# Order of the weight looks, turning steps of the second batch's x, and place of the third gated filler in an attention and ternary FFN kernel

## The chip, the cores and the metric

The kernel runs on one core of one Trainium2 chip. The metric is the device time of one execution in microseconds; each kernel is judged by the median of several timed runs. A separate execution was taken with the hardware profiler; its lines are quoted below. PE is the matrix engine, PEld its weight loads, DVE the vector engine, ACT the scalar engine, POOL the general engine, and SP the engine whose queue issues most of the DMA transfers.

## What is computed

The input x has 2 sequences of 2048 rows with 256 features, in fp32. One layer is computed, attention and FFN side by side on the normalised input:

```
xn = layernorm(x)
q, k, v = xn @ Wq, xn @ Wk, xn @ Wv
attn = softmax(causal(q @ k.T) * 256 ** -0.5) @ v @ Wo
h = silu((xn @ w1.T) * w1_s) * ((xn @ w2.T) * w2_s)      # 1024 wide
h = gelu((h @ h1.T) * h1_s)
h = gelu((h @ h2.T) * h2_s)
out = x + attn + (h @ w3.T) * w3_s
```

The FFN weights w1, w2, h1, h2 and w3 are ternary: each entry is -1, 0 or 1. The kernel doesn't assume this but looks at every weight, and has a second, general FFN for the case that a look finds something else.

## The kernel before

**Blocks.** The rows are cut into 8 blocks n of 512 rows (0 to 3 are the first sequence, 4 to 7 the second), each into 4 tiles t of 128 rows. Matmul operands are kept in two parts, a rounded high part and the remainder, the low part, so one product is three matmuls.

**Attention** runs first, tile by tile. `score(n, t, m)` (L428 to L449) multiplies tile (n, t) by the keys of block m, adds the causal mask (L434), takes the row maximum on DVE (L437) and, after the last m, the exponential on ACT (L449). The weights must then be transposed. Where at least five 128-column tiles lie together this is done off PE: a DVE transpose of 32x32 blocks into one of two b buffers (`turn_blocks`, L308), a DMA write to DRAM called d (L313), and four DMA fetches (`fetch_blocks`, L320) that put the blocks in place, into one of two buffers called e. `turn` then makes the high part (ACT, L487) and the low part (DVE or POOL in turn, L489) from e; otherwise it transposes on PE (L493). `weigh(n, t, m)` (L519, L524) multiplies by the values, and scales on ACT (L539) and adds on POOL (L540) after the last m.

**The order** of this work is written out by a planner. It counts each PE step in units of one matmul column group (a product of six 512-column matmuls is 3,072 units), goes through 34 steps j, and in step j merges the scores of tile j and the extra work listed for j with the weighing of an earlier tile. Steps 0 to 15 are the tiles of blocks 3 down to 0, steps 16 to 31 those of blocks 4 to 7; steps 32 and 33 only weigh. The tile framework then orders each engine's instructions by its own simulated time, so an instruction can run ahead of its place in the program; `issue_after` holds one behind another.

**Keys.** For the first sequence x is normalised and transposed on PE. For the second, `turn_keys(n)` does it ahead: four ACT activations normalise the block (L343), one DVE transpose (L308, x into b), one DMA write (d_x, L313) and four fetches back into x (L320) turn it. `keys(n)` later casts it into the key tile (ACT L366), subtracts the low part (POOL L367) and stores the keys to DRAM (xT_d, L368), from where the FFN loads them. `TURN_KEYS` lists the steps at which blocks 4, 5, 6 and 7 are turned. The queries (L385) and values (L401) of blocks 4 to 7 stand in steps 13 to 24.

**Looks.** Each of the FFN weights is looked at in pieces, beside the attention. The list `items` gives the order; `beside(cost)` runs the next step of the list when enough units have gone by since the last (the gap: 8,000 or 11,000 units where the next piece could be loaded ahead, 15,000 where not, because there are two staging buffers and a chunk of h1 takes both). A piece of w1, w2 or w3 takes a DVE bit test (L598) and an ACT sum (L600). A piece of h2 takes an absolute value on ACT (L605) and a comparison on DVE (L607). A chunk of h1 is two pieces: four sums of its quarters on DVE (L155), made in the tile xh0, a store of these (1024 KB, L621), and the test for both. After the last chunk of h1, xh0 is loaded with the keys of block 0 (L618). At attention's end `judge` (L502 to L506) brings all results into one flag, on which the branch to the FFN depends.

**Fillers.** The FFN's first products for block 0 read xh0 and need no attention result, so four of them are used to fill PE at attention's end: `first_quarter(i)`, i = 0 to 2 (8 matmuls at L174 into two PSUM banks, then silu on ACT L182, a product on DVE L183, and the split L187 and L188), and `last_quarter` behind attention's last matmul. The four banks `ps` are taken in turn by scores, fillers and the judge.

**FFN.** `ffn_ternary` goes through pairs of blocks. The two 1024x1024 layers are done by a seven-product scheme on quarters (L886), whose factors for h1 are the sums stored by the looks; the output product is L1047.

Of the kernel before, what the change touches and what calls it, by code (L numbers as in the profile page):

```python
# [21 lines left out]
TB = 512  # L22
NT = TB // P
# [5 lines left out]
Q = 32  # L29
UK = 8  # L30
LEAST = 5
TURN_KEYS = [8, 10, 12, 14]
LOOKS_FROM = 3
LEAD = 2
WARM = 26
# [30 lines left out]
def attn_ffn_kernel(  # L66
# [36 lines left out]
    B, S, D = x.shape  # L103
    H = w1.shape[2]
    NB = S // TB
    N = B * NB
    DC = D // P
    HC = H // P
    SC = 1024
# [81 lines left out]
    with ExitStack() as actx:  # L191
# [20 lines left out]
        def bank():  # L212
            return in_turn("ps", ps_tiles)
# [164 lines left out]
        def queries(n, m):  # L378
            if m == 0:
                qs[n] = in_turn("q", q_tiles)  # L380
            pp = bank()
            k = 0
            for a, b in ((0, 0), (1, 0), (0, 1)):
                for c in range(DC):
                    nc.tensor.matmul(  # L385
                        out=pp, lhsT=wqk[:, c, a, ts(m, P)], rhs=ks[n][:, c, b, :],
                        start=(k == 0), stop=(k == 3 * DC - 1),
                    )
                    k += 1
            hi_lo(qs[n][:, m, 0, :], qs[n][:, m, 1, :], pp)  # L390

        def values(n, half):
            if half == 0:
                vs[n] = vp.tile([P, NT, 2, D], F32R, tag="v", name=f"v_{n}")
            pv = bank().rearrange("p (u d) -> p u d", d=D)
            for u in range(2):
                t = 2 * half + u
                k = 0
                for c in range(DC):
                    for a, b in ((0, 0), (0, 1), (1, 0)):  # L400
                        nc.tensor.matmul(  # L401
                            out=pv[:, u, :], lhsT=ks[n][:, c, a, ts(t, P)], rhs=wvo[:, c, b, :],
                            start=(k == 0), stop=(k == 3 * DC - 1),
                        )
                        k += 1
            v = vs[n][:, ts(half, 2), :, :]
            hi_lo(v[:, :, 0, :], v[:, :, 1, :], pv)
# [90 lines left out]
        def judge():  # L498

            assert not looks  # L500
            most = small.tile([P, 1], F32, tag="most", name="most")
            nc.vector.reduce_max(most, low_bits[:, : looked[0]], axis=AX.X)  # L502
            with tc.issue_after(marks["PE"]):
                pf = bank()
                nc.tensor.matmul(out=pf[:1, :1], lhsT=most, rhs=ones, start=True, stop=True)
            nc.vector.tensor_copy(flag, pf[:1, :1])  # L506

        def weigh(n, t, m):
            if (n, t, m) == (N - 1, NT - 1, N - 1):
                judge()  # L510
            first = n - n % NB
            st = state[n, t]
            if m == first:
                st["po"] = ps_o.tile([P, 2, D], F32, tag="po", name=f"po_{n}_{t}")
            tiles = NT if m < n else t + 1
            pT = st.pop(m)

            for j in range(tiles):
                nc.tensor.matmul(  # L519
                    out=st["po"], lhsT=pT[:, 0, ts(j, P)], rhs=vs[m][:, j, :, :],  # L520
                    start=(m == first and j == 0), stop=False,
                )
            for j in range(tiles):
                marks["PE"] = nc.tensor.matmul(  # L524
                    out=st["po"][:, 0, :], lhsT=pT[:, 1, ts(j, P)], rhs=vs[m][:, j, 0, :],
                    start=False, stop=(m == n and j == tiles - 1),
                ).ins
            if m == n:
                total = small.tile([P, 1], F32, tag="total", name=f"total_{n}_{t}")
                nc.vector.reduce_sum(total, st["sums"][:, : (n - first) * NT // UK + 1], axis=AX.X)  # L530
                inv = small.tile([P, 1], F32, tag="inv", name=f"inv_{n}_{t}")
                nc.vector.reciprocal(inv, total)
                if n not in attn:
                    attn[n] = rp.tile([P, NT + 1, D], F32, tag="r", name=f"r_{n}"), []
                r, made = attn[n]

                up = n < NB
                two = r[:, ds(t, 2), :]
                nc.scalar.activation(two, st["po"], AF.Copy, scale=inv)  # L539
                nc.gpsimd.tensor_tensor(two[:, int(up), :], two[:, 0, :], two[:, 1, :], ALU.add)  # L540
                made.append(t)
                if len(made) == NT:
                    assert made == sorted(made, reverse=up)
                    nc.sync.dma_start(out=r_d[n], in_=r[:, ds(int(up), NT), :].rearrange("p t d -> p (t d)"))
                del state[n, t]
# [23 lines left out]
        def block_steps(n):  # L569
            return [  # L570
                (2 * TB, lambda: keys(n)),
                (6 * TB, lambda: queries(n, 0)),
                (6 * TB, lambda: queries(n, 1)),
                (6 * TB, lambda: values(n, 0)),
                (6 * TB, lambda: values(n, 1)),
            ]
# [15 lines left out]
        def low(tiles, dst):  # L592
            (t,) = tiles
            if dst is not None:
                rounded(dst, t)
            tb = t.bitcast(U32)
            with tc.issue_after(marks["DVE"]):
                nc.vector.tensor_scalar(tb, tb, LOW_BITS, None, ALU.bitwise_and)  # L598
            with tc.issue_after(marks["ACT"]):
                nc.scalar.activation(t, tb, AF.Copy, accum_out=seen())  # L600

        def odd(t):

            with tc.issue_after(marks["ACT"]):
                nc.scalar.activation(t, t, AF.Abs)  # L605
            with tc.issue_after(marks["DVE"]):
                nc.vector.scalar_tensor_tensor(  # L607
                    t, t, 0.0, t, ALU.not_equal, ALU.not_equal, accum_out=seen()
                )
# [19 lines left out]
        def item_low(src, dst):  # L629
            items.append(([src], [(0, lambda t: low(t, dst))]))  # L630

        def item_signs(src):
            items.append(([src], [(0, lambda t: odd(t[0]))]))

        def item_factors(src, f, c):
            steps = [(0, lambda t: sum_up(t, 0))]
            steps += [(2500, lambda t, i=i: sum_up(t, i)) for i in (1, 2, 3)]
            steps += [
                (1500, lambda t: store_sums(f, c)),
                (6000, lambda t: odd(t[0])),  # L640
                (3000, lambda t: odd(t[1])),
            ]
            if c == HK - 1:
                steps.append((0, lambda t: load_xh0()))
            items.append(([src[:, c, :], src[:, c + HK, :]], steps))

        for c in range(HK):
            src, dst = ((w1, w1_sb), (w2, w2_sb))[c // DC]
            item_low(src[:, c % DC, :], dst[:, c % DC, :])
        w3_at = list(range(0, HC, SC // D))  # L650
        for c in range(HK):
            item_factors(h1, factors["h1"], c)
            for k in (2 * c, 2 * c + 1):
                item_signs(h2[:, k, :])
            if c >= 2:
                w = w3_at[c - 2]
                item_low(w3[:, w : w + SC // D, :].rearrange("p c d -> p (c d)"), None)

        def fetched_weights(i):
            for src in items[i][0]:  # L660
# [50 lines left out]
        for k, src in (("w1", w1_s), ("w2", w2_s), ("h1", h1_s), ("h2", h2_s)):  # L711
# [3 lines left out]
        tiles = [divmod(i, NT) for i in range(NB * NT - 1, -1, -1)]  # L715
# [5 lines left out]
        extra = {  # L721
            0: [(6 * TB, lambda: values(0, 0)), (6 * TB, lambda: values(0, 1))],
            2: [(6 * TB, lambda: queries(2, 0)), (6 * TB, lambda: queries(2, 1))],
            6: [(6 * TB, lambda: queries(1, 0)), (6 * TB, lambda: queries(1, 1))],
            10: [(6 * TB, lambda: queries(0, 0)), (6 * TB, lambda: queries(0, 1))],
            13: block_steps(NB)[:3],
            14: block_steps(NB)[3:],
            15: block_steps(NB + 1)[:1],
            16: block_steps(NB + 1)[1:],
# [6 lines left out]
        def first_quarter(i):  # L736

            banks = [bank(), bank()]
            gated_products(banks, xh0, i)
            with tc.issue_after(marks["ACT"]):  # L740
                gated(f_views[i], banks, i)
                split_into(h_views[i], f_views[i])

        extra[len(tiles)] = [(8 * TB, lambda i=i: first_quarter(i)) for i in range(2)]
        extra[len(tiles) + 1] = [(8 * TB, lambda: first_quarter(2))]

        def before(j):
            if 3 <= j < 3 + NB:
# [4 lines left out]
            if j == 3 + NB:  # L753
                with tc.issue_after(marks["ACT"]):
                    r = root(mv1.rearrange("p n t k -> p (n t) k"), NB * NT, "1")
                for i in range(NB):
                    rstds[NB + i] = [a[:, ts(i, NT)] for a in r]
            if j in TURN_KEYS:
                turn_keys(NB + TURN_KEYS.index(j))

# [497 lines left out]
```

## Time and profile before

| What | Value |
|---|---|
| timed runs | 872.51, 873.72, 876.49 us (median 873.72) |
| the profiled execution | 870.29 us, of it the span 868.5 us |
| mean granted PE clock | 0.994 |
| busy in the span | PE 851.4 us, PEld 722.0, DVE 635.6, ACT 512.4, POOL 250.0 |
| DMA | 162.52 MB in 62,678 packets |
| steps 8, 16, 24, 31 scored (L434) at | 99.8, 140.1, 194.8, 254.8 us |
| x of blocks 4 to 7 normalised (first L343) at | 97.95, 117.53, 128.12, 136.81 us |
| the same cast into keys (first L366) at | 115.45, 131.52, 145.44, 158.53 us |
| h1's sums stored (L621) at | 100.37, 152.10, 186.12, 240.71 us |
| last matmul of attention; first FFN product in an own bank | 281.3; 283.2 us |

Times in the profile count from the span's start. In a list of instructions, the columns are the start, the time from the first start to the last end of the merged row, engine, line, operation, the names written and read, the count, and in brackets the idle time before it and what ended it. The busy time of PE includes matmuls that run at a lower granted clock. A stretch of a queue's own engine (SPq) is the time in which it issues.

### The profile page before, as it was taken

To read this page: it belongs to the slowest core of one execution; us is meant where nothing else is said; L and a number is where in the kernel's file an instruction comes from. 1 tells how busy PE (TensorE), PEld (TensorE's weight loads), DVE (VectorE), ACT (ScalarE), POOL (GpSimd) and SP (SyncE) were. 2 spreads that over 40 slices of the span, in tenths; PEclk is the share of its full clock that TensorE was granted. 3 is DMA by queue.
4 is the path that set the end of the run, shared out by engine and by line. 5 is a ranking of instruction groups with operands and counts; after the bars stand their busy time and mean duration, and the time that the engine had idled before them with its cause. 6 is when DMAs were issued, how large, how long until landed. Compare 5 with 4: busy or idle time off the path is not lost.

```text
span 868.5 us, 12281 instructions
## 1 busy us (share of the span) xinstructions
PE 851.4 (98%) x4298; PEld 722.0 (83%) x4298; DVE 635.6 (73%) x1091; ACT 512.4 (59%) x897; POOL 250.0 (29%) x194
## 2 busy tenths in 40 slices
PE   8999998999999999999999999999999999999997
PEld 6988877988887878888988888988888898888887
DVE  6688766776775699996596596579478648848764
ACT  3456677755647456677257586536557635657671
POOL 3033344321322576550142150025024003502300
PEclk9999999999999999999999999999999999999999
DMA  8977899765792998854234444433344431144411
GB/s 280 356 243 241 242 295 283 241 240 190 235 324 63 368 384 309 318 193 145 99 121 150 144 144 143 148 112 112 144 146 145 145 136 57 50 146 145 146 49 53
DMA packets 62678, 162.52 MB, mean 187 GB/s; under 512 B 6544, under 2 KB 36368, under 8 KB 53264
## 3 DMA queue, kind: packets, MB, share of 16 engines
q1 hardware_dynamic: 57792, 145.14, 48.1%
q10 hardware_dynamic: 3728, 12.32, 4.6%
q0 software_dynamic: 1088, 4.19, 1.3%
q8 instruction: 36, 0.59, 0.3%
q14 instruction: 34, 0.28, 0.1%
HBM read 120.21 MB, written 47.71 MB: 193 GB/s over the span
## 4 chain that ended last, share of the span: by engine, by line
PE 74%; DMA 11%; DVE 6%; issue 3%; SPq 2%; ACT 2%; POOL 0%; ACTq 0%; DVEq 0%; POOLq 0%
PE ps_own L886 23%; PE ps L886 22%; PE ps L174 6%; PE ps_own L174 6%; DMA e<-d 5%; PE ps_own L1047 4%; PE ps L1047 4%; PE ps L428 3%; SPq L320 2%; DMA d<-b 2%; PE po L519 2%; PE ps L401 2%; DMA x<-d_x 2%; DVE b L308 1%; PE ps L385 1%
## 5 line engine op out<-in xcount | busy, mean ns | idle before, releaser
L428 PE MATMUL ps<-k,q 128*128 128x512 f32 (+3 forms) x480 | 112.0, 368 | 0.4 <-ACT q L264 0.4
L428 PEld LDWEIGHTS ps<-k,q 128*128 128x128 f32 x480 | 82.5, 191 | 13.5 <-ACT q L264 1.2
L519 PE MATMUL po<-v,pT 128*128 128x512 f32 x272 | 79.4, 404 | 5.1 <-ACT pT L487 3.8
L1018 POOL TENSOR_TENSOR rt<-rt,xt 128x1024 f32<-128x1024 f32 x8 | 21.8, 2744 | 165.3 <-issue 114.8
L907 ACT ACTIVATE k_h_u<-k_h_u,h_s_sb 128x512 f32<-128x512 f32 x64 | 45.9, 723 | 38.5 <-DVE k_h_u L906 37.9
L449 ACT ACTIVATE s<-s,low 128x1024 f32<-128x1024 f32 (+7 forms) x48 | 43.0, 897 | 30.8 <-DVE low L443 30.7
L519 PEld LDWEIGHTS po<-v,pT 128*128 128x128 f32 x272 | 48.1, 191 | 14.0 <-ACT pT L487 4.9
L866 POOL TENSOR_TENSOR k_h_u<-k_h_p,k_h_u 128x512 f32<-128x512 f32 x16 | 23.2, 1452 | 122.8 <-ACT q L187 106.0
L489 POOL TENSOR_TENSOR pT<-e,pT 128x512 fp32r<-128x512 f32 (+3 forms) x30 | 36.2, 1205 | 64.8 <-ACT pT L487 59.6
L487 ACT CAST pT<-e 128x512 fp32r<-128x512 f32 (+3 forms) x60 | 32.5, 573 | 31.9 <-DMA e<-d 26.5
L540 POOL TENSOR_TENSOR r<-r 128x256 f32<-128x256 f32 x32 | 26.5, 829 | 82.9 <-ACT r L539 76.3
L437 DVE TENSOR_SCALAR_CACHE_REDUCE s<-ps 128x512 f32<-128x512 f32 (+3 forms) x80 | 47.2, 598 | 2.7 <-PE ps L428 1.6
L524 PEld LDWEIGHTS po<-v,pT 128*128 128x128 f32 x272 | 42.7, 191 | 7.3 <-DVE pT L489 1.1
L524 PE MATMUL po<-v,pT 128*128 128x256 f32 x272 | 47.7, 287 | 0.7 <-DVE pT L489 0.6
L188 DVE TENSOR_TENSOR q<-k_h_u,q 128x512 fp32r<-128x512 f32 x32 | 45.9, 1463 | 0.0
L308 DVE STREAM_TRANSPOSE b<-s 128x1024 f32<-128x1024 f32 (+3 forms) x30 | 33.7, 1130 | 13.8 <-ACT s L449 12.8
L925 POOL TENSOR_TENSOR k_h_p<-f_h_B,k_h_p 128x512 f32<-128x512 f32 x16 | 34.4, 2179 | 21.2 <-DVE h_h_T L188 21.2
L489 DVE TENSOR_TENSOR pT<-e,pT 128x512 fp32r<-128x512 f32 x30 | 23.4, 781 | 20.7 <-ACT pT L487 20.6
L174 PE MATMUL ps<-xh,w_sb 128*128 128x512 f32 x144 | 36.0, 391 | 1.7 <-ACT b L182 1.7
L866 POOL TENSOR_TENSOR f_w_B<-f_w_B,f_w_B 128x512 f32<-128x512 f32 x16 | 26.8, 1690 | 33.1 <-DVE f_w_B L183 33.1
L906 DVE TENSOR_TENSOR k_h_u<-ps_own,k_h_u 128x512 f32<-128x512 f32 x32 | 21.7, 686 | 17.6 <-PE ps_own L886 17.6
L907 ACT ACTIVATE k_h_p<-k_h_p,h_s_sb 128x512 f32<-128x512 f32 x32 | 22.8, 722 | 18.6 <-DVE k_h_p L906 18.6
(178 smaller groups left out, 2224.4 us busy)
## 6 DMA issues: line engine op xcount, KB each, us to landing
w_h_S<-factors_h SPq DMA_DIRECT2D x32, 1024.0 KB, 4.7
w_h_A<-factors_h SPq DMA_DIRECT2D x24, 1024.0 KB, 4.8
d<-b SPq DMA_DIRECT2D x18, 512.0 KB, 3.5
e<-d SPq DMA_DIRECT2D x72, 128.0 KB, 3.0
xT_d<-k SPq DMA_DIRECT2D x8, 1024.0 KB, 5.5
stg<-in_ffn_h_w ACTq DMA_DIRECT2D x16, 512.0 KB, 5.3
factors_h<-xh SPq DMA_DIRECT2D x4, 1024.0 KB, 4.9
r_d<-r SPq DMA_DIRECT2D x8, 512.0 KB, 5.3
```

What stands on the lines that cost most here:

```text
L174: nc.tensor.matmul(out=p, lhsT=w[:, c, ts(o, P)], rhs=xh[:, c, a, :], start=(c == 0 and a == 0), stop=(c == DC - 1 and a == 1),)
L188: nc.vector.tensor_tensor(r[:, 1, :], f, r[:, 0, :].bitcast(F32), ALU.subtract)
L428: nc.tensor.matmul(out=ps[:, :w], lhsT=qs[n][:, c, a, ts(t, P)], rhs=ks[m][:, c, b, :w], start=(k == 0), stop=(m < n and k == 3 * DC - 1),)
L437: marks["DVE"] = nc.vector.tensor_scalar(st["s"][:, ds(at, w)], ps[:, :w], 1.0, None, ALU.mult, ALU.max, accum_out=st["tops"][:, m - first ...
L449: marks["ACT"] = nc.scalar.activation(st["s"][:, at], st["s"][:, at], AF.Exp, bias=low, accum_out=st["sums"][:, u // UK : u // UK + 1],).ins
L489: engine.tensor_tensor(lo, src, hi.bitcast(F32), ALU.subtract)
L519: nc.tensor.matmul(out=st["po"], lhsT=pT[:, 0, ts(j, P)], rhs=vs[m][:, j, :, :], start=(m == first and j == 0), stop=False,)
L524: marks["PE"] = nc.tensor.matmul(out=st["po"][:, 0, :], lhsT=pT[:, 1, ts(j, P)], rhs=vs[m][:, j, 0, :], start=False, stop=(m == n and j == ...
L866: nc.gpsimd.tensor_tensor(B["B12"][i], B["B22"][i], B["B12"][i], ALU.subtract)
L886: nc.tensor.matmul(out=out[o], lhsT=w[:, c, ts(o, P)], rhs=sets[right][c][:, a, :], start=(start and c == 0 and a == 0), stop=(c == HK - 1 ...
L907: nc.scalar.activation(C[k][o], r[o] if r else banks[o], AF.Gelu, scale=s[:, at : at + 1])
L1047: nc.tensor.matmul(out=ys[t][:, :D], lhsT=h[c][:, a, ts(t, P)], rhs=w3_sb[:, c, :], start=(c == 0 and a == 0), stop=(c == HC - 1 and a == 1),)
```

## The change

Three things change.

1. `TURN_KEYS`: blocks 5, 6 and 7 are turned at steps 9, 10 and 12, where they were turned at 10, 12 and 14. Block 4 stays at 8.
2. The order of `items`: behind the four pieces of w1 and w2 come all eight pieces of h2, then the four chunks of h1, then the two pieces of w3. Before, each chunk of h1 was followed by two pieces of h2, and pieces of w3 stood after the third and the fourth group. The gaps follow from the order: between pieces of h2 the next is loaded ahead.
3. `first_quarter(2)` is called ahead of `weigh(7, 3, 6)`, the last but one; before, it was the first work of step 33, ahead of the weighing of tile (7, 2).

```diff
-TURN_KEYS = [8, 10, 12, 14]
+TURN_KEYS = [8, 9, 10, 12]
...
         def weigh(n, t, m):
+            if (n, t, m) == (N - 1, NT - 1, N - 2):
+                first_quarter(2)
             if (n, t, m) == (N - 1, NT - 1, N - 1):
                 judge()
...
         w3_at = list(range(0, HC, SC // D))
+
+        for k in range(HC):
+            item_signs(h2[:, k, :])
         for c in range(HK):
             item_factors(h1, factors["h1"], c)
-            for k in (2 * c, 2 * c + 1):
-                item_signs(h2[:, k, :])
-            if c >= 2:
-                w = w3_at[c - 2]
-                item_low(w3[:, w : w + SC // D, :].rearrange("p c d -> p (c d)"), None)
+        for w in w3_at:
+            item_low(w3[:, w : w + SC // D, :].rearrange("p c d -> p (c d)"), None)
...
         extra[len(tiles)] = [(8 * TB, lambda i=i: first_quarter(i)) for i in range(2)]
-        extra[len(tiles) + 1] = [(8 * TB, lambda: first_quarter(2))]
```

## The prediction

> **What bounds the kernel now.** I first read the busy time of each engine in stretches, cut where attention ends (281 us) and where each pair of FFN blocks ends.
>
> ```profile
> 88.00:281.00 193.00, 185.43 (x1024) 159.52 (x1024) 137.24 (x327) 124.09 (x235) 61.47 (x61) 0.98 0.75 237
> 424.00:570.00 146.00, 146.00 (x705) 123.28 (x704) 104.23 (x144) 87.18 (x146) 33.02 (x18) 1.00 0.39 137
> 716.00:862.50 146.50, 146.50 (x708) 123.58 (x706) 104.40 (x144) 86.01 (x145) 32.99 (x18) 1.00 0.27 94
> ```
>
> The columns are the stretch, its length, busy time (and count) of PE, PE's weight loads, DVE, ACT and POOL, then PE's granted clock, the DMA share and GB/s. From 424 us on PE never rests, and the diff touches nothing there. So the change can only win or lose PE's idle time and low clock between step 6 (73 us) and the first FFN products. The next view is the same, in finer stretches.
>
> ```profile
> 121.00:125.00 4.00, 2.91 (x13) 1.80 (x12) 3.11 (x8) 3.19 (x7) 0.73 (x1) 1.00 1.03 414
> 140.00:146.00 6.00, 6.00 (x35) 4.99 (x33) 3.10 (x8) 2.36 (x7) 1.71 (x3) 1.00 1.05 307
> 146.00:149.00 3.00, 0.35 (x2) 0.29 (x2) 0.48 (x2) 2.12 (x6) 2.86 (x3) 0.83 0.80 264
> 149.00:155.00 6.00, 6.00 (x25) 5.52 (x25) 5.07 (x15) 2.76 (x7) 1.89 (x3) 0.51 0.96 278
> 165.00:250.00 85.00, 84.72 (x471) 73.41 (x470) 65.56 (x168) 49.98 (x94) 23.48 (x23) 1.00 0.71 230
> 250.00:262.00 12.00, 11.46 (x59) 9.45 (x58) 6.16 (x14) 6.64 (x12) 3.15 (x4) 1.00 1.02 325
> 262.00:266.00 4.00, 2.31 (x15) 1.81 (x14) 2.19 (x6) 3.97 (x8) 0.00 (x0) 1.00 0.53 120
> ```
>
> One place stands out: an idle PE at 146 to 149, and half the clock for six microseconds behind it. To price low clock and short gaps too, I took the time from each matmul's start to the next, less the time that the same shape takes back to back (0.227 us for 512 columns, the 7.25 us per 32 of the FFN; 0.118 for 256). The excess is 2.78 us at 145.7 to 148.6, 2.93 behind it up to 155, 1.88 at 121 to 125, 2.45 in 165 to 250, 0.98 in 250 to 262, 1.74 in 262 to 266. That is nearly all there is to win. Now the queues at the worst place: PE, then ACT, then SP.
>
> ```profile
> 148.71 2.07 PE L519 MATMUL po<-v,pT 128*128 128x512 f32 x4 [2.65 <-ACT pT L487]
> ```
>
> ```profile
> 145.44 1.14 ACT L366 CAST k<-x 128x512 fp32r<-128x512 f32 x2 [3.64 <-DMA x<-d_x]
> 146.48 0.68 ACT L539 ACTIVATE r<-po,inv 128x512 f32<-128x512 f32 x1
> 148.04 0.82 ACT L487 CAST pT<-e 128x512 fp32r<-128x512 f32 x2 [0.88 <-DMA e<-d]
> ```
>
> ```profile
> 134.78 0.34 SPq L368 DMA_DIRECT2D xT_d<-k  x1
> 135.21 4.07 SPq L320 DMA_DIRECT2D x<-d_x  x4
> 139.32 0.49 SPq L544 DMA_DIRECT2D r_d<-r  x1
> 140.63 4.28 SPq L320 DMA_DIRECT2D e<-d  x4
> ```
>
> PE waits for a cast of turned weights, e. ACT first waits for turned x (block 6, turned at step 12), then for e. The fetch of e is late because on SP it stands behind block 5's key store, the four fetches of block 6's x and a result's store, while the DMA engines are full (1.05).
>
> **The change, part by part.** The profiled execution took 870.29 us (span 868.5); the median of the three timed runs is 873.72 (872.51 to 876.49). I sum against 870.29 and carry the difference over to the median.
>
> *Turning x at steps 8, 9, 10, 12.* A turn is four ACT activations (L343, 0.59 each, 2.06 as one row), one DVE transpose (1.24), one SP write of 512 KB and four SP fetches of 128 KB; when they land come two ACT casts (0.62 each), two POOL subtractions (1.42 each) and an SP store of 1024 KB. The planner's counts give block 5 its turn 14,080 units earlier, block 6 14,592, block 7 20,480; at 155 us per 305,152 units between steps 8 and 31 (scored 99.8 and 254.8) that is 7.2, 7.4 and 10.4 us. Block 6 thus takes block 5's old place, block 7 block 6's. The keys aren't needed earlier: their queries (L385) start 9 to 26 us behind the casts. No deadline is won, so what counts is what the transfers collide with.
>
> At 135 to 148 block 7 now stands where block 6 stood, with block 6's store ahead of it. What is gone from there are h1's two loads (issued at 134.96 and 137.55, 512 KB each; one load of h2 stands instead) and block 7's own write at 145. 512 KB less at 307 GB/s bring e in 1.7 us earlier, so 1.1 of the 2.78 us remain. Gaps of 1.07 and 1.70 us, at 123 and 265, left the clock at 1.00 in their stretches, so I take the low clock's 2.93 as gone: **-4.6**. Bounds: 0 (the collision stays) and -5.7 (gone altogether).
>
> The row is all that this rests on; a rule speaks against part of it. The Trainium skill, "TensorE: Matmul & The Clock Gate", section "HAM oscillation — how this bites in real kernels", has it that gaps over about 3.4 us throttle the clock. Here 2.65 us were enough, so by the measurement the gap's length alone doesn't decide. By the rule no gap of this trace would throttle, shortening one would save no clock, and the place would be worth 1.7 instead of 4.6.
>
> Block 5's turn at step 9 is a burst where there was none: ACT is 7.61 of 11 us busy there, the DMA share 0.87 to 0.95. The same burst at 117.5, with a look at 121, goes before the 1.88 us of 121 to 125; at 128 it cost nothing visible. Bounds 0 and +1.9; middle, **+1.0**. The casts and POOL's 2.83 us per block also move: POOL is busy 5.22 of 15 us from 125 to 140, so they cost nothing there; without that cover the lo half behind them (L489) is late by up to 2.83.
>
> *h2's looks first.* The looks' gaps add up to 332,000 units instead of 362,000. The last look is made in step 31 instead of 33, xh0 is loaded at 410,112 instead of 431,360, well before its first use in step 32, and h1's last store at 399,360 instead of 418,816; nobody waits for these. The 1 MB store of sums at 100.4 us moves behind step 16; block 5's x comes into that stretch instead. From step 16 on DVE has 16 sums, 8 odd tests and two low ones (11.0 + 9.8 + 1.6 us) in 216,000 units, where it had 8, 10 and two (5.5 + 12.2 + 1.6) in 271,000: 0.20 of the time instead of 0.14. DVE is at 0.77 from 165 to 250, and 0.9 between 230 and 250 cost PE nearly nothing; bounds 0 and +1.5, I take **+0.3**.
>
> *The end.* There ACT had, in one row, two exps, an abs of a look (1.04), a table load (1.28) and the silu (0.69):
>
> ```profile
> 262.18 1.04 ACT L605 ACTIVATE stg<-stg 128x1024 f32<-128x1024 f32 x1
> 263.24 1.28 ACT L182 ACT_TABLE_LOAD   x1
> 264.53 0.69 ACT L182 ACTIVATE b<-ps,w_s_sb 128x512 f32<-128x512 f32 x1
> 265.12 0.92 ACT L487 CAST pT<-e 128x512 fp32r<-128x512 f32 x2
> ```
>
> The third filler's PE work (8 x 0.227 = 1.8 us) waited 1.70 for a bank that this silu frees. Now the looks are over, and the filler, still 1.8 us of PE, comes behind 7,3,5, where PE lost 0.2 us in 17. What is late next is the cast at 265.12: without the abs it begins at 264.1, so PE still waits 0.8 (saved 0.9). The e fetch that lands for 271.28 is 1 us earlier, but PE, without the filler, comes there over 2 us earlier and gives up to 1.1 back. Against that stand the look's load at 257 that is gone from a full DMA (1.02, 0.98 us lost). Bounds -2.7 (1.74 + 0.98, both waits gone) and +1.1 (nothing saved, 1.1 lost); I take **-0.9**. The last filler, the judge and the branch to the FFN follow as before: PE is busy without a gap from 283 to 310.
>
> Sum: -4.6 + 1.0 + 0.3 - 0.9 = -4.2, so 866.1 for a profiled run, and on the median 873.72 - 4.2 = **869.5**.
>
> **Rivals.**
> *B, the wait only changes its name.* Block 7 takes block 6's place in front of the same fetch of e, and PE waits as long: 0 + 1.0 + 0.3 - 0.9 = +0.4, 874.1. For it: same step, same queue order. Against: 512 KB less in the way.
> *C, slower: a second collision.* Four turns fall into steps 8 to 12, where the DMA is at 0.87 to 1.03; block 5's transfers go on SP ahead of the e fetches of tiles (1,3) and (1,2), as block 6's did at 135. It decides once an e lands some 2.65 us behind PE's last ready work, between 110 and 135: then the gap and the low clock, 2.78 + 2.93 = 5.7, come on top of B: 879.8. Against: the store of sums at 100 is gone, which pays for one block's x.
> *D, all of it.* The collision and both waits at the end go, and the burst is hidden: -5.7 - 2.7 = -8.4, 865.3. Against: nothing moves e's own order on SP.
> That the looks' order does nothing at all is inside A and B, where it carries only +0.3.
>
> **How the numbers follow.** A (forecast) 0.40, D 0.15, B 0.25, C 0.20. About 0.5% (4.4 us) is what a measurement of this kernel can tell from no change. A lies 0.1 us from that edge, so half of it is faster; with nearly all of D that makes 0.35 faster. The other half of A and most of B: 0.43 same. C and a little of B: 0.22 slower. The likeliest case's own range is 866 to 873. The whole range goes from D, less the 1.2 us by which the lowest run lies under the median (864), to 878, a little short of C's centre: what is left out is about half of C and a little of D.
>
> **What would show it.** Right: in the changed profile no stretch at half the clock between 100 and 165, PE's longest wait there under 2 us, ACT's cast of k waiting for x under 3; PE's wait for the silu (L174 on L182) gone, a wait for pT near 265 in its place; attention's end (the first own-bank product, 283.2) about 4 us earlier, all FFN stretches as long as before. Wrong: half the clock still there behind a wait for pT (B), or earlier, behind (1,3) or (1,2) (C); PE waiting on DVE between 165 and 250 by more than 2 us above the 2.45 (the denser looks); or the FFN's first pair longer than 142.7 us, for then the late h1 factors matter after all.

## The result, and the profile after

The changed kernel took **877.97 us** (median of 10 runs, 875.00 to 884.58). The kernel before, beside it on the same chip, took 873.66 (10 runs, 871.84 to 876.49). The ratio is **1.0059**, 95% interval [1.0039, 1.0078], so the change made the kernel slower by about half a per cent. The forecast was 869.5.

The profiled execution took 878.34 us, of it the span 876.4. That is 8.0 more than the profiled execution before (870.29), where the medians differ by 4.3: the earlier execution lay below every timed run of its kernel. Differences between two profiles are therefore read for their place here, and the timed ratios for their size.

First the view that the prediction began with, busy time by stretches (the stretch, its length, busy time and count of PE, PEld, DVE, ACT and POOL, then PE's granted clock, DMA share, GB/s):

```profile
88.00:289.00 201.00, 186.70 (x1029) 160.42 (x1028) 139.94 (x329) 124.05 (x235) 64.32 (x61) 0.97 0.71 228
92.00:95.00 3.00, 0.56 (x3) 0.12 (x2) 0.92 (x3) 1.59 (x3) 0.00 (x0) 1.00 0.62 166
95.00:99.00 4.00, 3.87 (x12) 3.02 (x13) 2.69 (x8) 3.92 (x7) 3.26 (x3) 0.57 0.48 142
125.00:131.50 6.50, 0.31 (x2) 0.00 (x0) 1.50 (x3) 2.41 (x6) 1.72 (x2) 0.85 0.96 369
131.50:138.00 6.50, 6.39 (x20) 5.10 (x21) 5.74 (x15) 4.60 (x10) 3.68 (x3) 0.62 0.99 346
150.00:160.00 10.00, 10.00 (x65) 9.02 (x64) 5.39 (x18) 7.29 (x16) 5.58 (x6) 1.00 0.59 205
165.00:250.00 85.00, 79.57 (x434) 67.48 (x433) 64.09 (x160) 45.32 (x88) 21.92 (x22) 1.00 0.61 201
268.00:290.00 22.00, 22.00 (x128) 19.08 (x127) 9.84 (x19) 13.73 (x24) 6.65 (x7) 1.00 0.24 65
432.00:578.00 146.00, 146.00 (x705) 123.17 (x704) 104.31 (x144) 87.17 (x146) 33.01 (x18) 1.00 0.40 137
724.00:870.00 146.00, 146.00 (x705) 123.20 (x704) 104.35 (x144) 85.96 (x145) 32.99 (x18) 1.00 0.28 94
```

The FFN is what it was: 146 of 146 us in both stretches. The last matmul of attention ends at 289.7 instead of 281.3, so all of the loss lies in attention. The collision that stood at 146 to 155 is gone (step 16 is scored at 150.5 now instead of 140.1, and 150 to 160 is full), and so is the hole at the end (22.00 of 22.00). But there are two new holes, at 92 and at 125, each with half the clock behind it, and 165 to 250 lost 5.2 us of PE's busy time.

The hole at 92 comes from the new order of the looks. ACT stands 4.06 us at a look of h2 that waits for its load, and the cast of turned weights that PE waits for stands behind it:

```profile
93.41 1.06 ACT L607 ACTIVATE stg<-stg 128x1024 f32<-128x1024 f32 x1 [4.06 <-DMA stg<-in_ffn_h_w]
95.13 1.85 PE L521 MATMUL po<-v,pT 128*128 128x512 f32 x4 [2.57 <-ACT pT L487]
```

The excess that the prediction worked with (start to start, less the back-to-back time of the shape), summed between the scored steps (marked by L434), puts numbers to that. A stretch runs from its first step's L434 to that of the step behind its last, so the old wait at 146 lies in 10-16:

| Steps | 0-6 | 7-9 | 10-16 | 17-24 | 25-30 | 31 to the end | FFN |
|---|---|---|---|---|---|---|---|
| before, us | 6.90 | 1.56 | 8.50 | 1.62 | 1.70 | 2.89 | 3.00 |
| after, us | 7.59 | 4.67 | 10.07 | 4.33 | 4.92 | 0.03 | 2.95 |

The largest wait, by engine. First PE, then DVE and ACT (the list of instructions, with the idle time ahead of each and what ended it), then SP's own queue:

```profile
131.61 0.80 PE L428 MATMUL ps<-k,q 128*128 128x512 f32 x1 [6.30 <-DVE q L265]
```

```profile
129.09 1.14 ACT L366 CAST k<-x 128x512 fp32r<-128x512 f32 x2 [6.60 <-DMA x<-d_x]
130.00 0.98 DVE L308 STREAM_TRANSPOSE b<-s 128x768 f32<-128x768 f32 x1 [7.52 <-DMA d<-b]
130.71 0.57 ACT L264 CAST q<-ps 128x512 fp32r<-128x512 f32 x1
130.90 0.65 DVE L265 TENSOR_TENSOR q<-ps,q 128x512 fp32r<-128x512 f32 x1
```

```profile
110.81 0.38 SPq L313 DMA_DIRECT2D d<-b  x1
112.19 0.34 SPq L313 DMA_DIRECT2D d_x<-b  x1
118.98 1.74 SPq L320 DMA_DIRECT2D e<-d  x4
120.82 1.80 SPq L320 DMA_DIRECT2D x<-d_x  x4
122.72 0.38 SPq L313 DMA_DIRECT2D d<-b  x1
123.19 0.38 SPq L368 DMA_DIRECT2D xT_d<-k  x1
123.66 0.41 SPq L313 DMA_DIRECT2D d_x<-b  x1
```

Start with SP's queue, the last of the three. SP issued these in the order shown. The write of tile (1,3), issued at 110.81, landed at 118.84, and until then SP stood at the fetch of its e. Behind that come the four fetches of block 5's x, which now precede the write of tile (1,2). This write was issued at 122.72 and landed at 129.97; before, it was issued at 118.80 and landed at 122.02. Of these 7.95 us, 1.96 were lost already because (1,3)'s write landed later (at 116.88 before), as much again up to the issue, where the four fetches now stand, and 4.03 by the write's own slower landing. DVE needs the b buffer that this write reads, because block 6's turn took the other one, so DVE stands 7.52 us, and the low half of the queries (L265), which PE waits for, stands behind it. ACT stands nearly as long, 6.60 us, for block 5's x.

The other place lies in steps 25 to 30. ACT, and one row of DVE:

```profile
210.65 0.58 ACT L264 CAST v<-ps 128x512 fp32r<-128x512 f32 x1
219.04 0.62 ACT L487 CAST pT<-e 128x512 fp32r<-128x512 f32 x1 [7.81 <-DMA e<-d]
219.69 0.69 DVE L489 TENSOR_TENSOR pT<-e,pT 128x512 fp32r<-128x512 f32 x1 [5.19 <-ACT pT L487]
220.95 1.15 ACT L449 ACTIVATE s<-s,low 128x1024 f32<-128x1024 f32 x1 [1.29 <-DVE low L443]
222.59 1.14 ACT L449 ACTIVATE s<-s,low 128x1024 f32<-128x1024 f32 x1
230.72 1.14 ACT L487 CAST pT<-e 128x512 fp32r<-128x512 f32 x2 [4.05 <-DMA e<-d]
```

ACT stands 7.81 us at a cast of tile (6,0)'s turned weights. The exps of tiles (6,1) and (6,2) stand behind it, and DVE stands 5.19 us at the subtraction that follows the cast, with the last row maximum of (6,1) behind that. So the writes of these tiles go late, and their e is waited for in turn at 230.72. In the kernel before, the exps of (6,1) ran ahead of this cast:

```profile
204.51 1.15 ACT L449 ACTIVATE s<-s,low 128x1024 f32<-128x1024 f32 x1 [2.85 <-DVE low L443]
205.66 0.49 ACT L449 ACTIVATE s<-s,low 128x256 f32<-128x256 f32 x1
210.53 0.62 ACT L487 CAST pT<-e 128x512 fp32r<-128x512 f32 x1 [4.28 <-DMA e<-d]
211.97 1.15 ACT L449 ACTIVATE s<-s,low 128x1024 f32<-128x1024 f32 x1 [0.82 <-DVE low L443]
```

No line of the diff names this cast. The tile framework put it elsewhere, presumably because its own simulated time had shifted.

### The profile page after: what moved, and what is told of

Its sections match the earlier page's. It is cut to its first block, busy times and chain, and to the rows that moved or that the text cites. A ratio compares the mean times of both kernels' runs of the same rounds, so it can differ in the third digit from the quotient of the medians.

```text
span 876.4 us, 12282 instructions
## 1 busy us (share of the span) xinstructions
PE 853.1 (97%) x4298; PEld 722.5 (82%) x4298; DVE 636.2 (73%) x1091; ACT 513.1 (59%) x897; POOL 250.2 (29%) x194
## 4 chain that ended last, share of the span: by engine, by line
PE 78%; DMA 8%; DVE 5%; issue 4%; ACT 2%; SPq 1%; POOL 1%; ACTq 0%; DVEq 0%; POOLq 0%
PE ps_own L887 23%; PE ps L887 22%; PE ps L174 6%; PE ps_own L174 5%; PE ps L428 5%; DMA d<-b 4%; PE ps_own L1048 4%; PE ps L1048 4%; PE po L521 3%; DMA e<-d 2%; PE ps L401 2%; PE po L526 2%; DMA stg<-in_ffn_h_w 2%; SPq L320 1%; PE ps L385 1%
## 5 line engine op out<-in xcount | busy, mean ns | idle before, releaser
L489 DVE TENSOR_TENSOR pT<-e,pT 128x512 fp32r<-128x512 f32 x30 | 27.1, 902 | 19.9 <-ACT pT L487 19.6
L174 PE MATMUL ps<-xh,w_sb 128*128 128x512 f32 x144 | 36.3, 390 | 0.0
```

The lines of the kernel that those rows point to most:

```text
L174: nc.tensor.matmul(out=p, lhsT=w[:, c, ts(o, P)], rhs=xh[:, c, a, :], start=(c == 0 and a == 0), stop=(c == DC - 1 and a == 1),)
L489: engine.tensor_tensor(lo, src, hi.bitcast(F32), ALU.subtract)
```

## The experiments

Line numbers are those of the kernel in question (in after, those from 510 to 650 stand two higher than before). The times:

| Kernel | What it is | us, median (range) | ratio to before [95%] |
|---|---|---|---|
| after | the change | 877.97 (875.00-884.58) | 1.0059 [1.0039, 1.0078] |
| e1 | before + turns | 874.60 (873.40-877.78) | 1.0005 [0.9986, 1.0024] |
| e2 | before + looks | 872.10 (870.87-876.27) | 0.9980 [0.9957, 1.0003] |
| e3 | before + filler | 874.63 (871.25-878.25) | 1.0007 [0.9989, 1.0025] |
| e4 | after, turns undone | 873.27 (870.50-874.99) | 0.9979 [0.9960, 0.9999] |
| e5 | after, filler undone | 877.80 (875.90-882.29) | 1.0042 [1.0024, 1.0060] |
| e6 | after, x in b buffers of its own | 876.60 (874.57-879.64) | 1.0032 [1.0014, 1.0049] |
| e7 | e4, x in b buffers of its own | 872.47 (869.41-874.86) | 0.9978 [0.9960, 0.9995] |
| e8 | after, block 5's fetches behind (1,2)'s write | 874.84 (870.88-877.08) | 1.0005 [0.9988, 1.0023] |
| e9 | after, only block 5 early | 873.94 (871.68-878.50) | 1.0013 [0.9995, 1.0031] |
| e10 | after, only blocks 6 and 7 early | 872.81 (867.43-875.57) | 0.9986 [0.9969, 1.0004] |
| e11 | after, the cast of (6,0) behind the exps | 872.41 (868.24-877.44) | 0.9983 [0.9964, 1.0003] |
| e12 | e8 and e11 together | 871.77 (870.45-876.02) | 0.9981 [0.9970, 0.9993] |

Each ratio is to runs of the kernel before on the same chip (medians 875.08 beside e1 to e4, 874.18 beside e5 to e8, 873.68 beside e9 to e12). It is not the quotient of the two medians, from which it differs by up to 0.0014, so differences of that size between kernels say nothing. And the excess by steps in the profiled execution of each, in us, with where the cast of (6,0) stands on ACT to the exps of (6,1) and (6,2):

| Kernel | 7-9 | 10-16 | 17-24 | 25-30 | end | cast |
|---|---|---|---|---|---|---|
| before | 1.56 | 8.50 | 1.62 | 1.70 | 2.89 | between |
| after | 4.67 | 10.07 | 4.33 | 4.92 | 0.03 | ahead |
| e1 | 1.14 | 9.86 | 0.92 | 1.58 | 3.77 | between |
| e2 | 4.86 | 8.49 | 3.93 | 0.88 | 0.03 | behind |
| e3 | 1.37 | 7.75 | 2.41 | 2.32 | 3.04 | between |
| e4 | 1.98 | 8.62 | 4.75 | 0.88 | 0.38 | behind |
| e5 | 3.13 | 10.15 | 4.22 | 5.43 | 0.27 | ahead |
| e6 | 2.41 | 8.95 | 4.46 | 4.92 | 0.03 | ahead |
| e7 | 4.48 | 7.32 | 3.91 | 0.88 | 0.98 | behind |
| e8 | 1.79 | 7.78 | 4.40 | 5.61 | 0.03 | ahead |
| e9 | 1.60 | 9.38 | 6.11 | 0.85 | -0.01 | behind |
| e10 | 3.93 | 8.65 | 0.90 | 0.91 | 1.30 | behind |
| e11 | 4.61 | 8.74 | 1.81 | 0.84 | 1.57 | behind |
| e12 | 1.49 | 7.70 | 3.92 | 0.83 | 0.10 | behind |

How far one profile can be trusted is in this table too. e2 and e4 run the same order on every engine up to the fillers at the end, and lost 4.86 and 1.98 us in steps 7 to 9. After and e11 run the same up to about step 26, and lost 4.33 and 1.81 in steps 17 to 24. A phase's number from one execution is good to some 3 us.

**Each edit alone (e1, e2, e3) and the turns taken back (e4).**

```diff
# e1: the kernel before, with
-TURN_KEYS = [8, 10, 12, 14]
+TURN_KEYS = [8, 9, 10, 12]
# e2: the kernel before, with the change's order of items (all h2, then h1, then w3)
# e3: the kernel before, with first_quarter(2) ahead of weigh(7, 3, 6)
# e4: the changed kernel, with
-TURN_KEYS = [8, 9, 10, 12]
+TURN_KEYS = [8, 10, 12, 14]
```

> Only the turning steps are changed (8, 9, 10, 12). Theory 1 (the collision of the closer turns is the whole loss): the wait of PE on DVE behind the b buffer at 125 us is there (6 us, half the clock behind it), the old wait at 146 is gone, and the time is 4 us above before (ratio 1.005). Theory 2 (the places add up: 110 to 165 us changed by +0.4 only, the loss is made by the looks at 92 us and after 165): the same wait, but 874, ratio 1.000 within 0.002. Theory 3 (each edit reshuffles the whole order that the framework draws up, and the parts don't add): anything, with waits at places that neither kernel has.

> Only the order of the looks is changed. Theory 1: within 0.002 of before, the wait at 146 us stays. Theory 2: ACT waits some 4 us for a piece of h2 near 90 us and PE 2.6 us behind it with a low clock (+3.8), the stretch from 165 to 250 loses 6 us more than before, attention's end gains 2: +8 us, ratio 1.009. Theory 3: neither.

> Only the third filler is moved. Up to 255 us the profile is that of before. My prediction had the wait at 265 us shrink from 1.74 to 0.8 and up to 1.1 given back: without the looks' end, 0 to -1 us, ratio 0.999 to 1.000. If the filler's move makes attention's end in the changed kernel (2.7 us less lost) by itself: -2.5 us, 0.997.

> The changed kernel with the turns back at 8, 10, 12, 14. Theory 1: the wait at 125 us goes, the one at 146 comes back smaller; 4 to 6 us under the changed kernel, ratio to before 0.998 to 1.000. Theory 2: 110 to 165 costs the same, so within 1 us of the changed kernel, ratio 1.006. Theory 3: neither.

No edit alone costs time that can be measured: 1.0005, 0.9980 and 1.0007. Without the turns the change is at 0.9979. So the loss belongs to turns and looks together. e1 did not gain at the old collision either. PE stands there 3.13 us, now behind the low half of the values on DVE, with half the clock from 145.1 on for 6.8 us:

```profile
145.77 4.63 PE L385 MATMUL ps<-k,wqk 128*128 128x512 f32 x10 [3.13 <-DVE v L265]
```

The wait changed its name, as rival B had it, though it is not B's fetch of e. In e4, DVE waits for a b buffer as in the change, for 4.32 us, and the kernel is still level with before or a little faster:

```profile
124.68 0.98 DVE L308 STREAM_TRANSPOSE b<-s 128x768 f32<-128x768 f32 x1 [4.32 <-DMA d<-b]
126.35 1.43 PE L428 MATMUL ps<-k,q 128*128 128x512 f32 x5 [4.01 <-DVE q L265]
```

The gain at the end, 2.89 to 0.03, comes with the looks alone (e2) and not with the filler alone (e3, 3.04). The hole at 92 comes with the looks too: in all eleven kernels with the new order ACT stands 2.21 to 4.26 us there for a load of h2, and steps 7 to 9 lose 1.49 to 4.86 (1.14 to 1.56 in the three with the old order). Since e2 as a whole is not slower than before, it is not what makes the change lose.

**Turns and looks without the filler (e5), and x in b buffers of its own (e6, e7).**

```diff
# e5: the changed kernel, with first_quarter(2) back at the head of step 33
# e6: the changed kernel, e7: e4, each with
+    xb = const.tile([P, 2, DC * TB], F32, tag="xh0", name="xb")
...
-            b = in_turn("b", b_tiles).rearrange("p i t -> p (i t)")[:, : k * P]
+            if name.startswith("x"):
+                b = xb[:, int(name[2:]) % 2, :]
+            else:
+                b = in_turn("b", b_tiles).rearrange("p i t -> p (i t)")[:, : k * P]
# and xh0 made at step 15, in the same place
```

> The changed kernel without the filler's move. By the first four runs neither edit costs anything alone, and turns with looks are the pair that can: 876 to 878, ratio 1.004 to 1.007, with PE's wait behind DVE and b near 125 us. If the filler is needed for the loss: 1.000 within 0.002.

> The changed kernel with turned x in two halves of xh0, which nobody uses before step 17, in place of the two b buffers; the transfers and their order on SP at 100 to 130 us stay. Theory b (the transpose of tile (1,1) holds DVE until (1,2)'s write has left the b buffer, because x and scores take turns in two of them): DVE's 7.5 us wait on d<-b goes, PE's 6.3 with the low clock too, the time falls by 6 to 9 us, ratio to before 0.995 to 0.999. Theory DMA (the transfers are too many for 100 to 130 us, whoever waits): PE waits for pT from e instead, ratio 1.004 to 1.006.

> e4 (turns at 8, 10, 12, 14, looks and filler as changed) with turned x in xh0. Theory b: the waits on d<-b (6.4 us on DVE, 4.2 on PE at 122 us, half the clock for 3.4 us behind it) go: 4 to 5 us under e4, ratio 0.993 to 0.995, faster than both kernels. Theory DMA: 0.998 as e4.

e5 loses like the change (1.0042), with a wait of PE of 5.83 us before 132.63: the filler is not part of it. By ratios, turns (1.0005) and looks (0.9980) would give 0.9985 together; they give 1.0042, so 0.57% (5.0 us) are interaction. e6 keeps the order of the change on PE and took DVE's wait for a b buffer away. Yet PE still stands 3.91 us (6.30 in after), because block 5's x is late as well:

```profile
127.51 1.14 ACT L370 CAST k<-x 128x512 fp32r<-128x512 f32 x2 [5.00 <-DMA x<-d_x]
129.76 2.08 PE L432 MATMUL ps<-k,q 128*128 128x512 f32 x4 [3.91 <-ACT q L265]
```

So the shared buffer is one of two waits that end close together, not the whole cause. e6's 1.0032 lies between what the two theories asked for, and e7 is level with e4, as theory DMA had it.

**Block 5's x fetches behind (1,2)'s write (e8).**

```diff
-            turned_keys[n] = fetch_blocks(turn_blocks(xn, NT * DC, f"x_{n}"), NT * DC, xn)
+            d = turn_blocks(xn, NT * DC, f"x_{n}")
+            if n == NB + 1:
+                held.append(lambda: turned_keys.update({n: fetch_blocks(d, NT * DC, xn)}))
+                return
+            turned_keys[n] = fetch_blocks(d, NT * DC, xn)
...
+                        if (n, t) == (1, 2):
+                            for fetch in held:
+                                with tc.issue_after(marks["d"]):
+                                    fetch()
```

> The changed kernel with block 5's four fetches of x held on SP behind the write of tile (1,2), which they stood ahead of. If the place on SP makes the wait: that write is issued near 120 instead of 122.7 us, DVE's wait on d<-b falls from 7.5 to the 4.5 of e2 and e4, the time by 3 to 4 us, ratio 1.001 to 1.003. If not: 1.006.

SP now issues (1,2)'s write at 120.40, ahead of the fetches at 120.93. DVE's wait for it is 0.93 us, and PE's longest wait there is another one, half as long:

```profile
124.27 2.07 PE L529 MATMUL po<-v,pT 128*128 128x512 f32 x4 [3.04 <-ACT pT L495]
```

The time falls from 1.0059 to 1.0005; the intervals are apart. Steps 25 to 30 still lose 5.61. But the framework drew up a different order on PE, DVE and ACT too, at many places from 130 us on. So that the fetches' place on SP makes the whole gain is not shown.

**Which early turn, and the cast (e9 to e12).** The theories are counted anew in these four: 1 is the pairing of b buffers, 2 block 5's fetches ahead of the write, 3 the place of the cast.

```diff
# e9:  TURN_KEYS = [8, 9, 12, 14]
# e10: TURN_KEYS = [8, 10, 11, 12]
# e11: the changed kernel, e12: e8, each with
                     ).ins
+                    marks[n, t] = marks["ACT"]
...
-                nc.scalar.copy(hi, src)
+                if (n, t, m) == (6, 0, 4):
+                    with tc.issue_after(marks[6, 2]):
+                        nc.scalar.copy(hi, src)
+                else:
+                    nc.scalar.copy(hi, src)
```

> The change with TURN_KEYS = [8, 9, 12, 14]: of the three blocks that the change turns earlier, only block 5 is. Its x fetches still stand on SP ahead of (1,2)'s write, but no turn of block 6 lies between tiles (1,2) and (1,1), so these two no longer share a b buffer. Theory 1 (the pairing of b buffers, made by block 6's turn at step 10): DVE's wait for d<-b near 125 us under 1 us, planner steps 10 to 16 back to 8.0 to 8.8 us of excess, 872 to 874.5 us. Theory 2 (block 5's fetches ahead of the write are enough): PE still waits 3 us or more between 120 and 132 us, 876 to 878 us. Steps 25 to 30: ACT's cast of pT (6,0) stands behind the exps of (6,1) and (6,2) here, so theory 3 (that cast's place costs 4 us) expects an excess of 0.9 to 2 us there, and its rival (three turns so early fill the DMA queues later too) 4 us or more.

> The change with TURN_KEYS = [8, 10, 11, 12]: block 5 where it was before the change, blocks 6 and 7 early. (1,2)'s write stands ahead of block 5's turn on SP, as with the turns undone (e4). Theory 1 (pairing alone): block 5's turn now lies between (1,2) and (1,1) as in e4, DVE waits 4 to 5 us for d<-b, 873 to 875 us. Theory 2 (block 5's fetches ahead of the write): no such fetch is ahead, 871 to 873.5 us, PE's longest wait between 110 and 135 us under 3 us. Theory 3: cast behind the exps, steps 25 to 30 at 0.9 to 2 us. If instead early turns as such cost, 876 us or more.

> The change with one cast held: ACT's cast of pT of tile (6,0) (which waits for its e) is put behind the exps of (6,1) and (6,2), as it stands in all kernels without the loss in steps 25 to 30; the rest of the order is as in the change. Theory 3 (that cast's place in ACT's order costs steps 25 to 30 their 4.92 us): excess there 0.9 to 2 us, 873.5 to 875 us in all. Rival (the e of (6,0) and what follows are late anyway, since SP and DMA are behind): 4 us or more stays, 877 to 878.5 us. The waits near 125 us stay in either case (PE over 5 us).

> The change with both: block 5's x fetches behind (1,2)'s write on SP (as e8), and the cast of pT of (6,0) behind the exps of (6,1) and (6,2) (as e11). If the two losses are separate, e8's 874.84 less some 4 us: 870 to 872 us, which would be below the kernel before (874) and level with or below e4 and e7. If a loss taken away at one place comes back at another, 873.5 to 875.5 us.

*e9.* The wait for a b buffer near 125 is gone, as theory 1 had it, but PE still stands 4.77 us (theory 2: 3 or more), behind ACT's cast of block 5's x:

```profile
124.98 1.14 ACT L366 CAST k<-x 128x512 fp32r<-128x512 f32 x2 [4.92 <-DMA x<-d_x]
127.23 2.07 PE L428 MATMUL ps<-k,q 128*128 128x512 f32 x4 [4.77 <-ACT q L264]
```

Theory 1 falls as the sole cause, as in e6. Yet the kernel takes 873.94 us where theory 2 asked for 876 to 878: the wait near 125 alone does not make the loss. The cast stands behind the exps here, and steps 25 to 30 lose 0.85.

*e10.* With block 5 where it was, no wait of PE between 110 and 135 reaches 2 us (1.57 at most); the next one, 3.44 at 148, is a chain over a look that waits for its load. Its ratio is 0.9986, and the time and the missing wait are as theory 2 asked. Turning blocks 6 and 7 early costs nothing that can be measured.

*e11.* One cast was moved: 872.41, where theory 3 asked for 873.5 to 875 and its rival for 877 or more. Up to the cast the order is that of the change, but behind 219 us the framework moved other work too, on PE at some ten places; the cleaner comparison is e12 with e8. The wait near 125 is still there (4.69 us), and steps 25 to 30 lose 0.84. ACT now does the exps first, and finds e landed when it comes to the cast:

```profile
212.31 1.15 ACT L449 ACTIVATE s<-s,low 128x1024 f32<-128x1024 f32 x1 [4.63 <-DVE low L443]
213.95 1.14 ACT L449 ACTIVATE s<-s,low 128x1024 f32<-128x1024 f32 x1
215.69 0.61 ACT L490 CAST pT<-e 128x512 fp32r<-128x512 f32 x1
222.21 1.14 ACT L492 CAST pT<-e 128x512 fp32r<-128x512 f32 x2 [1.84 <-DMA e<-d]
```

*e12.* Against e8 its engines' orders differ in this cast, and in the DVE subtraction behind it, and in nothing else. The medians are 874.84 and 871.77, the phase 5.61 and 0.83, as theory 3 has it. Over all fourteen profiles the phase loses 4.92 to 5.61 with the cast ahead, 1.58 to 2.32 with it between and 0.83 to 0.91 with it behind: no overlap. That the place of this cast, with its subtraction, costs some 4 us there is shown (4.78 between the profiles of e8 and e12). In the whole time it is less certain: 3.07 between these two medians, 2.1 by the ratios, whose intervals overlap a little.

The 871.77 of e12 lies in the range set for separate losses. Yet the two repairs do not add up: 1.0059 becomes 1.0005 with one, 0.9983 with the other and 0.9981 with both. So either of them takes away most of the loss, and the second adds little. Why isn't settled; the 3 us of chance in a phase would hide it in these profiles. e4, e7 and e12 have their intervals below 1, about 0.2% under the kernel before. The filler and the early turns add nothing that can be measured to what the looks alone give (e2, 0.9980).

## Why the prediction was wrong

*The collision (-4.6).* The prediction read the place rightly and the balance wrongly. The wait at 146 and its half clock did go. But "I take the low clock's 2.93 as gone: **-4.6**" is the step that failed: it held the collision for a sum that can be taken out. With the turns alone (e1) the terms -4.6 and +1.0 would have given 3.6 us less; measured was 1.0005, 0.4 us more, with an interval of -1.2 to +2.1. Steps 10 to 16 lost 8.50 us before and 10.07 after, and 7.3 to 10.2 in each of the fourteen kernels, however the turns and looks were ordered. So a wait that was taken away at one tile came up at another. Between 105 and 150 us the DMA share is 0.86 to 1.01 in all fourteen (0.93 before, 0.94 after); that the full DMA engines are the reason is likely, but no run lessened the bytes, so it is not shown.

*The sum itself.* The prediction added the parts up as if each kept its price beside the others. The three edits alone measured +0.05, -0.20 and +0.07%, and turns and looks together lose 0.57% (5.0 us) more than their sum. For that there was no term.

*Block 5's turn at step 9 (+1.0).* The bounds, 0 and +1.9, came from how busy ACT and the DMA are there. What stands on SP behind the moved fetches was named only in rival C. They are ahead of (1,2)'s write, and in after PE stood 6.30 us behind that write's buffer, with half the clock behind it. How much of this the fetches' place alone made isn't settled: the write's issue was 1.96 us later already for another reason, and e8, which put the write ahead, changed more than that.

*Rival C* had the place (110 to 135), the mechanism (block 5's transfers in the way on SP) and nearly the size (879.8; 877.97 measured). It was wrong in the object: PE waited for no e there; a write was issued late, and its b buffer held DVE and the queries, while block 5's x held ACT. And it was not all of the loss, as e11 shows, which has that wait and is as fast as the kernel before.

*h2's looks first (+0.3).* The term looked from step 16 on only, and "nobody waits for these" left out the looks of h2 themselves: one of them made the hole at 92. PE's loss between 165 and 250 did rise above the bound set for it, from 0.28 idle us to 5.43. But the denser looks are not shown to be the cause: with the same looks, steps 17 to 24 lost 0.90 and 1.81 in e10 and e11, 3.9 to 6.1 in others. What is shown, in steps 25 to 30, is the cast of (6,0), for which the prediction had no term at all. It assumed that an engine's order away from the edit stays as it was.

*The end (-0.9).* The right sign, and mis-sized: 2.89 became 0.03. L174 no longer waits for the silu, and the wait for pT near 265 that the prediction expected in its place did not come. Of its bounds, -2.7 and +1.1, the lower one came. It came with the looks: the end lost -0.01 to 1.57 us in the eleven profiles with the new order and 2.89 to 3.77 in the three with the old one, of which e3 has the moved filler. So the filler is not what made it.

*Of the list of what would show it*: half the clock between 100 and 165 is there (129.6 us, for 6.8), PE's longest wait is 6.30 instead of under 2, ACT's cast of k waits 6.60 instead of under 3, attention ends 8.4 us later instead of 4 earlier. The wait for the silu is gone and the FFN as long as before, as the prediction said.

## What to carry to other kernels

Price a step that is moved earlier by what stands behind it on each in-order queue, not by how busy the engines are there: find the first instruction that it now precedes, and who waits for that one's result and its buffer. Where a framework orders the instructions by a simulated time, compare the whole order on each engine after an edit; here a cast and its subtraction, waiting for a DMA ahead of other work, cost some 4 us near 219 us, while the turns, by which alone e4 and the change differ, begin before 140. And where the DMA engines are full, be slow to book a wait that disappears as a gain: here the loss of the stretch stayed between 7.3 and 10.2 us however the transfers were ordered.

## What the runs showed of the hardware

**The clock looks at fixed windows.** Where a run has two stretches of half clock in attention, their starts lie whole multiples of 3.413 us apart, in all seven runs that have two (34.1 us in after, 102.4 in e8, 54.6 in e10, for example), and each is one or two such windows long (3.4 or 6.8 us). I laid windows of that length from the start of the first one through each of the fourteen traces and took PE's idle share in each. In the windows at full clock with half clock behind them PE was idle 0.47 to 1.00 of the window; the highest share without half clock behind it was 0.55. So it is about half of a window's time, summed over its gaps, that decides: in e10 a wait of 1.80 us lay in one window and cost the clock; in before the wait of 1.70 near 263 lay across two and did not. The half clock lasted for a second window where PE was idle for 0.19 to 1.00 of the first, and it ended after windows with 0.10 or less. The Trainium skill, "TensorE: Matmul & The Clock Gate", section "What's actually happening", tells of a free-running window of 3413 ns, which these runs bear out; the rule in its section "HAM oscillation — how this bites in real kernels", to have no idle gaps of PE over about 3.4 us, is not strict enough here, 1.80 us being enough in e10.

**A write's time from issue to landing varied.** (1,2)'s write of 448 KB took 3.22 us before (issued at 118.80, landed at 122.02) and 7.25 us after (122.72 to 129.97), behind four fetches of x and beside a 1024 KB store and another write. In e8, issued ahead of those fetches at 120.40, it took 7.17. That the other transfers under way make the difference is likely, but not shown.

**Work stands behind a waiting head.** In after, SP stood until 118.98 at the fetch of (1,3)'s e while the store of block 4's keys, which it issued at 123.19, had its data from 116.42 on. DVE stood until 130.00 at a transpose, with a subtraction of the queries behind it whose cast was done at 121.97. In e8, ACT stood until 213.86 at the cast of (6,0) while the exp of (6,1) behind it had its last input from 210.55 on. The Trainium skill, "Perfetto Trace Analysis", section "Tensor Engine Instruction (MATMUL, LD_WEIGHTS)", calls ACT and DVE strict FIFO, and no row here speaks against it.
